# A four-layer graph network on one core: the second layer's parts in one format, its comparisons on another engine, and odd-sized transfers in two

## Chip, cores and metric

The kernel runs on one core of a Trainium2 chip. The metric is device time in microseconds (us) of one execution. The kernel before has a median of 3609.15 us over 3 runs (3607.2 to 3612.18).

The core's engines are named as in the profile: PE (matrix products; PEld is its weight load), DVE (the vector engine), ACT (the scalar engine), POOL (GpSimd) and SP, which here issues transfers. DMA moves data between memory and the on-chip buffers. PSUM is the memory that PE writes its results to.

## What is computed

There are N = 3327 nodes with 512 features, and an adjacency matrix `adj` of N x N. Three attention layers and one aggregation layer follow each other; each reads a normalised, rectified copy of x and is added to x:

```python
h = jnp.maximum(_layernorm(x, axis=-1), 0.0)
x = x + layer(h, adj, ...)
# an attention layer (layers 0 and 2 have 8 heads of 64, layer 1 has 4 heads of 128):
Wh = h @ W                                  # per head
e = leaky_relu(s1[i] + s2[j], 0.2)          # s1, s2: Wh times a vector, per head
attention = softmax(where(adj > 0, e, -inf), over j)
out = elu(attention @ Wh)
# layer 1 alone also sets the diagonal of the mask
# the last layer: mean of the neighbours' features, two dense products, relu
```

## The kernel before

**Tiles.** The nodes make 26 tiles of 128; the last has 127. Targets go in 7 chunks of four tiles (the last chunk has two), sources in five groups `JG` of 6, 6, 6, 4 and 4 tiles.

**Attention without an exponential per edge.** exp(leaky_relu(s1 + s2)) is a product of a factor of the target and a factor of the source, with one pair of factors where s1 + s2 > 0 and another where it is not. So for each head the kernel compares s1 of the chunk's targets with -s2 of every source tile (128 x 512 at a time), which gives a matrix of ones (written as 2.0 in fp8). With the mask it is split into two matrices of edges, and each is multiplied on PE with the source features scaled by the fitting factor (called a = 0 and a = 1). The two sums are scaled per target by `L.c`, added and divided by the last column.

**Where the comparisons run.** In L650 to L657 ACT does them with a huge slope and a Relu (L656), except for the tiles listed in `GP_ON_DVE` (L46), which DVE does (L653): 3 tiles of 26 in the first layer, 8 in the second, 5 in the third. DVE then makes the first matrix by a bitwise "and" with the mask (L662) and the second by an exclusive "or" (L666, in the second layer L722, in place, once the first one has been used).

**Parts.** PE's inputs are split so that the sum keeps float32 accuracy. In layers 0 and 2 the features are three bf16 parts side by side (195 columns, L694 and L697). In the second layer (l = 1) `KIND = "bssvv"` says how each source group goes: group 0 with three bf16 parts (387 columns, L690) and the fp8 matrix as it is; groups 1 to 4 with two float32r parts (258 columns, L687), for which the fp8 matrix is first copied to float32r by `real` (L585): by ACT into buffers "ts" (three of them) for the groups marked s, by DVE into "tv" (two of them) for those marked v. The parts are made by `pieces` or `parts` while the layer before runs, stored to memory and loaded for each head ("ab").

**Order of the second layer.** For each chunk and head: load the scores and parts, make the matrices, then for a = 0 and 1 two passes. A pass takes two target tiles through all 26 source tiles into two of the four accumulators. After a pass DVE reduces the three parts of each accumulator into R (L708; the third is zero where only two were made), and `hooks.run` (L718) lets a step of the next layer's node work in: load x, statistics, normalise, transpose, project, scale, split, store. After the last pass R is multiplied by `L.c` (L730), summed (L732), and divided (L734 to L737).

**Start.** Before the first attention product all 26 tiles are normalised, projected and split (`node_stages` with first=True). x is loaded by SP six tiles ahead (L833), the first layer's weights by SP too (L290), and 20 mask tiles are transposed on PE (L221), written to memory and loaded back (`load_mask`, `mask_tiles`). Then the first head's matrices are made.

**End.** The last layer multiplies the mask with float32r features (L921), adds and stores one tile of `out` at a time (L932).

An order is kept by hand in places: `after(inst, name)` tells the scheduling layer that one instruction is to be placed behind another. All engines take their own instructions in order.

Of the kernel before, what the change touches and what calls it, by code (L numbers as in the profile page):

```python
# [29 lines left out]
FP8 = mybir.dt.float8e4  # L30
F32R = mybir.dt.float32r
# [6 lines left out]
P = 128  # L38
EPS = 1e-5
SLOPE = 0.2  # L40
S_MIN = 1e-35
BIG = 2.0 ** 30
# [3 lines left out]
GP_ON_DVE = [(5, 12, 19), tuple(range(18, 26)), (4, 9, 14, 19, 24)]  # L46


KIND = "bssvv"
# [3 lines left out]
def tile_gnn(ctx: ExitStack, tc: tile.TileContext, x, adj, W0, a01, W1, al, ar, W2, a2,  # L53
# [48 lines left out]
    s1d = [dram.tile([NT, H, P], F32, name=f"s1_{l}") for l, H in enumerate(heads)]  # L102
# [10 lines left out]
    for l in range(3):  # L113
        H, DA, AO, HW = dims(l)
        if l == 1:
            abd.append([dram.tile([H, 2, P, nj, AO], BF16, name=f"ab{l}_{g}") if KIND[g] == "b" else
                        dram.tile([H, 2, P, nj, 2 * DA], F32, name=f"ab{l}_{g}") for g, (_, nj) in enumerate(JG)])
        else:
            abd.append([dram.tile([H, P, nj, HW], BF16, name=f"ab{l}_{g}") for g, (_, nj) in enumerate(JG)])
# [28 lines left out]

    stored = {}
    gone = []  # L150
# [52 lines left out]
    def load_mask(pool, t, g):  # L203


        hooks.done += 1
        n = pn(t)
        c, k = where[t]
        j0, nj = JG[g]
        w = min(nj * P, N - j0 * P)  # L210
        at = pool.tile([P, JM * P], BF16, name="at", bufs=3)
        if n < P:
            nc.vector.memset(at, 0.0)
        elif w < nj * P:
            nc.vector.memset(at[:, w:nj * P], 0.0)
        ld = nc.gpsimd.dma_start(at[:n, :w], adj[t * P:t * P + n, j0 * P:j0 * P + w])
        if gone:
            after(ld, gone[-2] if len(gone) > 1 else stored[NT - 1])
        tp = ps.tile([P, 8, P], BF16, name="tp", bufs=2)
        for j in range(nj):  # L220
            tr = nc.tensor.transpose(tp[:, j, :], at[:, j * P:(j + 1) * P], identb)  # L221
            if j == 0 and gone:
                after(tr, gone[-1])
        st = pool.tile([P, JM, P], FP8, name="st", bufs=3)
        nc.vector.tensor_scalar(st[:, :nj], tp[:, :nj], 0.0, 2.0, op0=ALU.is_gt, op1=ALU.mult, saturate=False)
        if j0 <= t < j0 + nj:
            d = pool.tile([P, P], BF16, name="d", bufs=1)
            nc.vector.tensor_tensor(d, tp[:, t - j0, :], negI, ALU.is_gt)
            nc.vector.tensor_scalar(dg1[:, t, :], d, 2.0, None, op0=ALU.mult, saturate=False)
        nc.sync.dma_start(maskd[c][g][:, k], st[:, :nj])  # L230

    def mask_tiles(c, self_loops=False, early=False):
        t0, nt = chunks[c]
        tiles, loops = [], []
        for g, (j0, nj) in enumerate(JG):
            m = mk.tile([P, PER * JM * P], FP8, name="m")
            v = m[:, :nt * nj * P].rearrange("p (k j i) -> p k j i", k=nt, j=nj)
            ld = nc.sync.dma_start(v, maskd[c][g])
            if early and c == 0:
                after(ld, stored[21])  # L240
            if self_loops:
                for k in range(nt):
                    if j0 <= t0 + k < j0 + nj:
                        loops.append((v[:, k, t0 + k - j0, :].bitcast(U32), dg1[:, t0 + k, :].bitcast(U32)))
            tiles.append(v)
# [17 lines left out]
    def open_layer(l):  # L263
# [17 lines left out]
        for i in range(2):  # L281
            av.append(pre.tile([P, 2, H2, DK], F32, name="h"))
            ld = nc.sync.dma_start(av[i].rearrange("p f h d -> p (f h) d"), a_srcs[l][i].partition_broadcast(P))
            if l:
                after(ld, stored["gate"])
        for k in range(KC):
            for f in range(2):
                dst = L.w[:, k, f, :D // 2]
                if l == 0:
                    nc.sync.dma_start(dst.rearrange("p (g o) -> p g o", g=H2),  # L290
# [6 lines left out]
        def fold(i, k):  # L297
# [3 lines left out]
            if gone:  # L301
                after(m, gone[-1])
            nc.vector.tensor_reduce(L.w[:, k, :, D // 2 + i * H2:D // 2 + (i + 1) * H2], pr, AX.X, ALU.add)
        folds = [lambda i=i, k=k: fold(i, k) for i in range(2) for k in range(KC)]
        if l:
            hooks.small = folds
        else:
            for f in folds:
                f()
# [18 lines left out]
    def normed(xt, mv, pool, behind=None):  # L328
        h = pool.tile([P, D], F32, name="h", bufs=2)
        act = nc.scalar.activation(h, xt, AF.Relu, bias=mv[:, 3:4], scale=mv[:, 2:3])  # L330
        if behind:
            after(act, behind)
        return h
# [7 lines left out]
    def pieces(L, t, AB, pool, first, behind=None):  # L341
# [6 lines left out]
        if o == 0:  # L348
            L.pt = pool.tile([P, H, 2, two, AO] if l == 1 else [P, H, two, HW], BF16, name="pt", bufs=3 if first else 2)
        pt = L.pt  # L350
        nc.gpsimd.memset(pt[:, :, :, o, 3 * DA:AO] if l == 1 else
                         pt[:, :, o].rearrange("p h (a w) -> p h a w", a=2)[..., 3 * DA:AO], 1.0)

        def dst(s, a):
            if l == 1:
                return pt[:, :, a, o, s * DA:(s + 1) * DA]
# [14 lines left out]
        if o == two - 1 and l == 1:  # L371
            for a in range(2):
                L.to_store.append((abd[l][g][:, a, :, js, :].rearrange("h p j w -> p h j w"), pt[:, :, a]))
        elif first and o == two - 1:
# [4 lines left out]
    def projected(L, t, hT, first):  # L379
# [4 lines left out]
        pws = []  # L384
        for f in range(2):
            pw = (accs if first else ps).tile([P, D // 2 + H], F32, name="acc" if first else "mm")
            for k in range(KC):
                L.mm = nc.tensor.matmul(pw, hT[:, k, :], L.w[:, k, f, :], start=(k == 0), stop=(k == KC - 1)).ins.name  # L388
# [3 lines left out]
            pws.append(pw)  # L392
# [19 lines left out]
    def parts(L, t, AB, pool, first, behind=None):  # L412
# [5 lines left out]
        if l == 1 and KIND[g] != "b":  # L418
# [17 lines left out]
    def project_last(L, t, hT, i, behind=None):  # L436
# [10 lines left out]
        if i == 0:  # L447
            def add():
# [4 lines left out]
                nc.sync.dma_start(y1d[c][kk * P:kk * P + n, :], y[:n])  # L453
# [10 lines left out]
    def send_s1(L, t, pool, first):  # L464
# [10 lines left out]
        (nc.sync if first else nc.gpsimd).dma_start(s1d[L.l][t0:t0 + nt].rearrange("t h p -> (t h) p"), s1t[:nt * H])  # L475

    def node_stages(L, t, get_x, pool, first=False):
# [7 lines left out]
        def statistics():  # L485
            q["mv"] = norm(q["x"], pool, behind())
# [21 lines left out]
        if first:  # L508
            return [lambda: (q.update(x=get_x()), statistics(), relu()), turn,
                    lambda: parts(L, t, scaled(L, t, projected(L, t, q["hT"], first), pool, first), pool, first), send]  # L510
# [82 lines left out]
    ahead = {}  # L593

    def load_pieces(L, pool, g, h):
# [4 lines left out]
        v = tl[:, :nj * HW].rearrange("p (j w) -> p j w", j=nj)  # L600
        return v, nc.sync.dma_start(v, abd[L.l][g][h])

    def attention(L, hooks, open_next, close):
# [4 lines left out]
        masks = mask_tiles(0, l == 1, l == 0)  # L608
        for c, (t0, nt) in enumerate(chunks):
            W = nt * P  # L610
# [3 lines left out]
            for h in range(H):  # L614
# [8 lines left out]
                s1b = rp.tile([P, WMAX], F32, name="s1b", bufs=2)  # L623
                nc.sync.dma_start(s1b[:, :W].rearrange("p (k i) -> p k i", k=nt), s1d[l][t0:t0 + nt, h, :].partition_broadcast(P))
                ab = []
                for a in range(2 if l == 1 else 1):
                    row = []
                    for g, (_, nj) in enumerate(JG):
                        if l == 1:
                            tl = mp.tile([P, JM * 2 * DA], F32R, name="ab", bufs=7)  # L630
                            two = KIND[g] != "b"
                            w = 2 * DA if two else AO
                            v = (tl if two else tl.bitcast(BF16))[:, :nj * w].rearrange("p (j w) -> p j w", j=nj)
                            ld = nc.sync.dma_start(v.bitcast(F32) if two else v, abd[l][g][h, a])
                        else:
                            v, ld = ahead.pop(g) if g in ahead else load_pieces(L, mp if l else bp, g, h)
                        row.append(v)
                    ab.append(row)
                if c == 0 and h == 1:
                    stored["gate"] = ld.ins.name  # L640
                    N_ = open_next()
                s1v = s1b[:, :W].rearrange("p (k i) -> p k i", k=nt)
                th, flip = [[], []], []
                for g, (j0, nj) in enumerate(JG):
# [740 lines left out]
```

## Time and profile before

| | us |
|---|---|
| median of 3 runs | 3609.15 |
| the profiled execution | 3609.94 |
| its span, first to last instruction | 3608.10 |
| PE busy | 3470.2 (96%) |
| DVE busy | 2648.6 (73%) |
| ACT busy | 2511.8 (70%) |
| POOL busy | 603.0 (17%) |
| first attention product, layer 0 | at 185.07 |
| first product of the second layer | at 1278.0 |
| last product of the second layer | at 2119.4 |
| last matrix product of all | at 3591.7 |

All numbers of the profile come from one execution, and times in it count from the start of its span. A line of the timeline gives start, length, engine, source line, operation, what is written and read, the size and the number of instructions merged in it; in brackets stands how long the engine was idle before it and what ended that. Lengths of instructions that follow each other overlap by some hundredths of a microsecond, so a rate is read from start to start. A table by stage gives the busy time of each engine in that stretch.

### The profile page before, as it was taken

Reading aid. Unit: us, or ns where it says so; the run is one execution under the profiler, and the core shown is the slowest. Engines: PE = TensorE matmul, PEld = TensorE weight load, DVE = VectorE, ACT = ScalarE, POOL = GpSimd, SP = SyncE. Lnnn points to the kernel's source line nnn. Section 1 sums busy time; section 2 is a strip of 40 time slices with the busy share of each in tenths; the row PEclk is TensorE's granted clock in tenths of the full one; section 3 lists DMA queues with packets and bytes.
Section 4 is the critical chain, followed back from the end, with each engine's and each line's share of the span. In section 5 each row is a group of like instructions: output and inputs, shape, how many; then the busy total and the mean of one; then the engine's idle time right before and its main releaser. Section 6 shows DMA issues by size and latency. Waiting matters only on the chain. (4 is left out here: it accounts for less than half of the span.)

```text
span 3608.1 us, 78551 instructions
## 1 busy us (share of the span) xinstructions
PE 3470.2 (96%) x31291; PEld 3131.4 (87%) x31291; DVE 2648.6 (73%) x5227; ACT 2511.8 (70%) x4113; POOL 603.0 (17%) x855
## 2 busy tenths in 40 slices
PE   6799999999999999999999989999999999999998
PEld 5589999999999878888888869989898989876886
DVE  7688888888887779888888868867676768672211
ACT  5587787777787788888788767767676767572111
POOL 6511221111110111233222230001010101010000
PEclk9899999999999999999999999999999999999999
DMA  7687777878866877877777876655555555576331
GB/s 213 213 239 219 212 217 215 229 207 234 237 194 206 297 264 272 286 254 277 278 257 271 311 265 205 194 176 181 175 191 182 169 176 189 169 270 253 101 104 52
DMA packets 369431, 780.69 MB, mean 216 GB/s; under 512 B 35906, under 2 KB 207333, under 8 KB 368416
## 3 DMA queue, kind: packets, MB, share of 16 engines
q1 hardware_dynamic: 341024, 713.17, 59.4%
q0 software_dynamic: 28032, 62.41, 7.3%
q8 instruction: 249, 4.08, 0.4%
q14 instruction: 126, 1.03, 0.1%
HBM read 667.96 MB, written 129.64 MB: 221 GB/s over the span
## 5 line engine op out<-in xcount | busy, mean ns | idle before, releaser
L694 PE MATMUL acc<-ab,tht 128*128 128x195 bf16 (+1 forms) x10816 | 1840.4, 248 | 15.6 <-DVE tht L662 14.3
L697 PE MATMUL acc<-ab,gt 128*128 128x195 bf16 (+1 forms) x10816 | 1839.4, 248 | 6.6 <-DVE rc L734 4.3
L656 ACT ACTIVATE gt<-s1b,ks 128x512 fp8e4<-128x512 f32 (+1 forms) x2464 | 1457.4, 677 | 316.5 <-issue 158.6
L694 PEld LDWEIGHTS <-tht 128*128 128x128 fp8e4 x10816 | 1059.1, 98 | 28.9 <-DVE tht L662 15.9
L697 PEld LDWEIGHTS <-gt 128*128 128x128 fp8e4 x10816 | 1058.9, 98 | 26.5 <-issue 20.2
L662 DVE TENSOR_TENSOR tht<-gt,m 128x768 uint32<-128x768 uint32 (+3 forms) x560 | 447.4, 799 | 141.4 <-ACT gt L656 139.5
L666 DVE TENSOR_TENSOR gt<-tht,m 128x768 uint32<-128x768 uint32 (+3 forms) x560 | 448.9, 802 | 8.7
L590 ACT CAST ts<-tht 128x1536 fp32r<-128x1536 fp8e4 x208 | 300.3, 1471 | 55.9 <-PE acc L687 51.7
L687 PE MATMUL acc<-ab,ts 128*128 128x258 f32 x2496 | 334.2, 290 | 4.4 <-ACT ts L590 2.3
L653 DVE TENSOR_SCALAR gt<-s1b,ns 128x512 fp8e4<-128x512 f32 (+1 forms) x448 | 222.2, 501 | 149.6 <-PE acc L697 147.9
L687 PEld LDWEIGHTS acc<-ab,ts 128*128 128x128 f32 x2496 | 314.1, 191 | 13.4 <-ACT ts L590 3.0
L921 PE MATMUL acc<-y,mf 128*128 128x512 f32 x1352 | 309.8, 391 | 1.6 <-DVE mf L916 1.6
L656 ACT ACTIVATE tht<-s1b,ks 128x512 fp8e4<-128x512 f32 (+1 forms) x504 | 308.5, 681 | 2.8 <-DMA s1b<-s 2.3
L921 PEld LDWEIGHTS acc<-y,mf 128*128 128x128 f32 x1352 | 253.5, 188 | 57.8 <-DVE mf L916 2.0
L712 DVE TENSOR_REDUCE R<-acc 128x130 f32<-128x390 f32 x416 | 214.5, 555 | 91.6 <-PE acc L697 91.0
L797 POOL TENSOR_TENSOR xt<-xt,e 128x512 f32<-128x512 f32 x72 | 122.2, 1697 | 888.8 <-DVE e L796 567.5
L690 PE MATMUL acc<-ab,tht 128*128 128x387 bf16 x1248 | 226.1, 329 | 6.0 <-DVE tht L662 3.2
L918 ACT CAST mf<-m 128x768 fp32r<-128x768 fp8e4 (+1 forms) x78 | 59.1, 762 | 245.1 <-PE acc L921 233.3
L687 PE MATMUL acc<-ab,tv 128*128 128x258 f32 x1664 | 220.0, 283 | 3.3 <-DMA ab<-ab 2.2
L687 PEld LDWEIGHTS acc<-ab,tv 128*128 128x128 f32 x1664 | 207.5, 189 | 6.2 <-issue 2.1
L388 PE MATMUL mm<-w,hT 128*128 128x260 f32 (+1 forms) x832 | 198.4, 393 | 9.3 <-ACT hT L141 5.6
L690 PEld LDWEIGHTS <-tht 128*128 128x128 fp8e4 x1248 | 117.3, 98 | 83.3 <-DVE tht L662 3.6
(141 smaller groups left out, 3421.4 us busy)
## 6 DMA issues: line engine op xcount, KB each, us to landing
ab<-ab SPq DMA_DIRECT2D x336, 600.0 KB, 5.6
ab<-ab SPq DMA_DIRECT2D x224, 400.0 KB, 4.1
ab<-ab SPq DMA_DIRECT2D x112, 774.0 KB, 6.3
ab<-ab SPq DMA_DIRECT2D x112, 516.0 KB, 5.5
ab<-ab SPq DMA_DIRECT2D x56, 582.0 KB, 6.6
s1b<-s SPq DMA_DIRECT2D x120, 256.0 KB, 6.2
m<-mask SPq DMA_DIRECT2D x72, 384.0 KB, 4.2
ab<-pt SPq DMA_DIRECT2D x13, 1600.0 KB, 7.6
```

The costliest lines, as they stand in the source:

```text
L388: L.mm = nc.tensor.matmul(pw, hT[:, k, :], L.w[:, k, f, :], start=(k == 0), stop=(k == KC - 1)).ins.name
L590: (nc.scalar.copy if KIND[g] == "s" else nc.vector.tensor_copy)(t[:, :k1 - k0, :nj], th[a][g][:, k0:k1])
L653: nc.vector.tensor_scalar(gv[:, :, jj, :], s1v, L.ns2[:, j, h:h + 1], 2.0, op0=ALU.is_gt, op1=ALU.mult, saturate=False)
L656: nc.scalar.activation(gv[:, :, jj, :], s1v, AF.Relu, bias=L.ks2[:, j, h:h + 1], scale=BIG, saturate=False)
L662: nc.vector.tensor_tensor(pu, gu, mu, ALU.bitwise_and)
L666: nc.vector.tensor_tensor(gu, pu, mu, ALU.bitwise_xor)
L687: mm = nc.tensor.matmul(acc[k][:, :2 * DA], thr[g][:, k - ks[0], jj, :], ab[a][g][:, jj, :], start=(j == 0), stop=(j == NT - 1), skip_grou ...
L690: mm = nc.tensor.matmul(acc[k][:, :3 * DA], th[a][g][:, k, jj, :], ab[a][g][:, jj, :3 * DA], start=(j == 0), stop=(j == NT - 1), skip_grou ...
L694: nc.tensor.matmul(acc[k][:, :3 * DA + o], th[0][g][:, k, jj, :], ab[0][g][:, jj, :3 * DA + o], start=(j == 0), stop=False, skip_group_che ...
L697: mm = nc.tensor.matmul(acc[k][:, AO:AO + 3 * DA + o], th[1][g][:, k, jj, :], ab[0][g][:, jj, AO:AO + 3 * DA + o], start=False, stop=(j == ...
L712: nc.vector.tensor_reduce(R[:, k], v.rearrange("p a (s d) -> p a d s", s=3), AX.X, ALU.add)
L921: nc.tensor.matmul(acc[k], mf[:, jj, :], y2[g][:, jj, s, :], start=(j0 + jj == 0 and s == 0), stop=(j0 + jj == NT - 1 and s == 1))
```

## The change

1. **One format in the second layer.** `KIND` becomes "vssvv": group 0 has two float32r parts like the others. `real` makes its float32r matrix on DVE in a "tv" buffer; these stay two and grow from 4 to 6 source tiles each. The "tht" buffers of that layer go from 10 to 9. `parts`, the stores and the loads follow.
2. **Sums scaled out of PSUM.** In the second layer the reduce, the product with `L.c` and the sum are replaced by two operations for each accumulator, which scale each part by the target's factor and add it to R. `close_terms`, which makes the factors, comes before the first of them.
3. **Comparisons.** In the second layer the eight source tiles that DVE compared become tiles 1, 4, 7, 10, 13, 16, 19, 23, and POOL compares them. It writes the byte 64, which read as fp8 is 2.0.
4. **Transfers of 127 rows.** `move` issues a transfer of a row count that 16 does not divide as two: 112 and 15 rows here. It is used for loads of x, for y1, for the last layer's rows and for the store of `out`.
5. **Start.** The first chunk's masks are written straight into the buffers that attention reads, group by group; a mask tile's load is issued one step before its transposes. x is loaded by ACT's queue from the third tile on, half of the first weights too, and the statistics of the first two tiles come before the products with the attention vectors. Tiles 0 and 1 are projected first without their score columns. The first head's parts are copied on the chip into the buffers that attention reads. The first head's scores are loaded and the matrices of groups 0 to 2 made during the projections (`early`).
6. **Next layer's weights** are opened at the fourth head of the first chunk instead of the second, in layers 0 and 2.

The core of the diff:

```diff
-GP_ON_DVE = [(5, 12, 19), tuple(range(18, 26)), (4, 9, 14, 19, 24)]
-KIND = "bssvv"
+ELSEWHERE = [(5, 12, 19), (1, 4, 7, 10, 13, 16, 19, 23), (4, 9, 14, 19, 24)]
+KIND = "vssvv"
...
+    def move(eng, to, src, n):
+        m = n - n % 16
+        ld = eng.dma_start(to[:m], src[:m])
+        return [ld] if m == n else [ld, eng.dma_start(to[m:n], src[m:n])]
...
+            if j in ELSEWHERE[l] and l == 1:
+                nc.gpsimd.tensor_scalar(gv[:, :, jj, :].bitcast(U8), s1v, L.ns2[:, j, h:h + 1], TWO,
+                                        op0=ALU.is_gt, op1=ALU.mult, saturate=False)
+            elif j in ELSEWHERE[l]:
+                nc.vector.tensor_scalar(gv[:, :, jj, :], s1v, L.ns2[:, j, h:h + 1], 2.0,
+                                        op0=ALU.is_gt, op1=ALU.mult, saturate=False)
...
                             if l == 1:
-                                nc.vector.tensor_reduce(R[:, k, a, :], acc[k][:, :3 * DA].rearrange("p (s d) -> p d s", s=3),
-                                                        AX.X, ALU.add)
+                                cf = L.c[:, t0 + k, a, h:h + 1]
+                                for s in range(2):
+                                    v = acc[k][:, s * DA:(s + 1) * DA]
+                                    if a == s == 0:
+                                        nc.vector.tensor_scalar(R[:, k, 0, :], v, cf, None, op0=ALU.mult)
+                                    else:
+                                        nc.vector.scalar_tensor_tensor(R[:, k, 0, :], v, cf, R[:, k, 0, :],
+                                                                       op0=ALU.mult, op1=ALU.add)
...
-                Rv = R[:, :nt]
-                nc.vector.tensor_mul(Rv, Rv, L.c[:, t0:t0 + nt, :, h:h + 1].to_broadcast([P, nt, 2, DA]))
-                nc.vector.tensor_add(num[:, :nt], Rv[:, :, 0, :], Rv[:, :, 1, :])
+                if l != 1:
...
-            [A[1], ("ab", JM * 258, F32R, 7), R, ("ts", 2 * JM * P, F32R, 3), ("tv", 2 * 4 * P, F32R, 2), tht[:3] + (10,)],
+            [A[1], ("ab", JM * 258, F32R, 7), R, ("ts", 2 * JM * P, F32R, 3), ("tv", 2 * JM * P, F32R, 2), tht[:3] + (9,)],
...
-                nc.sync.dma_start(xt[:pn(u)], x_rows(0, u))
+                for ld in move(nc.scalar if u > 1 else nc.sync, xt, x_rows(0, u), pn(u)):
+                    if relus:
+                        after(ld, relus[-1])
...
+            for g in range(3):
+                if n == (8, 15, 21)[g]:
...
+                    pv, gv, _, steps = matrices(L, PER, 0, g, early["s1"], masks0[g], b[:, :s], b[:, s:2 * s])
+                    hooks.small += steps
+                    early[g] = pv, gv
...
-                    nc.sync.dma_start(out[t * P:t * P + n, :], o[:n])
+                    move(nc.sync, out[t * P:t * P + n, :], o, n)
```

## The prediction, made before the changed kernel was run

> **What bounds the kernel now.** I read the page's table of 40 slices first, then busy time by stage, then PE's timeline inside the second layer, then what waits at the two ends of the run. By stage (start to first attention product, layer one, layer two, layer three, aggregation, tail):
>
> ```profile
> 0.00:185.00 185.00, 128.97 (x631) 104.48 (x631) 121.51 (x253) 105.52 (x223) 110.94 (x193) 0.92 0.71 211
> 185.00:1278.00 1093.00, 1065.51 (x11933) 1037.34 (x11933) 904.18 (x1844) 858.50 (x1514) 174.56 (x273) 0.99 0.77 225
> 1278.00:2120.00 842.00, 826.36 (x5943) 719.78 (x5944) 729.63 (x1373) 705.91 (x964) 206.61 (x230) 0.99 0.79 279
> ...
> 3592.00:3608.00 16.00, 0.00 (x0) 0.00 (x0) 1.19 (x2) 0.00 (x0) 0.00 (x0) 0.62 0.06 19
> ```
>
> The columns are the stretch, then busy us of PE, weight loads, DVE, ACT and POOL, then granted clock, DMA share, GB/s. PE is busy 98% of layer two (826 of 842 us) and DVE 87%: PE is the bound, DVE is close behind. The first 185 us and the last 16 us are not PE-bound. One pass (two target tiles, 26 source tiles) of layer two:
>
> ```profile
> 1613.84 2.14 PE L690 MATMUL acc<-ab,tht 128*128 128x387 bf16 x12
> 1615.68 3.19 PE L687 MATMUL acc<-ab,ts 128*128 128x258 f32 x24
> 1618.71 2.08 PE L687 MATMUL acc<-ab,tv 128*128 128x258 f32 x16
> 1620.63 2.15 PE L690 MATMUL acc<-ab,tht 128*128 128x387 bf16 x12
> ```
>
> From start to next start a pass is 6.79 us. The 16 "tv" products start 0.120 apart (1.92/16). At 0.120 for all 40 float32r products, the 12 bf16 ones take 6.79 - 4.80 = 1.99, or 0.166 each.
>
> **Layer two on PE.** The 1248 bf16 products of 387 columns become float32r ones of 258. At 0.120 a pass is 52 x 0.120 = 6.24: 0.55 less. Read the other way, by the "ts" spacing (3.03/24 = 0.126), the 12 take 1.51 instead of 1.84: 0.33 less. There are 26 tiles / 2 x 4 heads x 2 parts = 104 passes, so 34 to 57 us; single starts in the middle of each run are 0.164 and 0.120 apart, which gives 0.52 a pass. I take **-54 us** of PE time.
>
> **Layer two on DVE, per head of four tiles.** The window 1400 to 2000 holds 19 heads (152 "tv" copies, 8 a head) of 31.6 us; DVE is busy 525.7 us in it, 27.7 a head. Durations below are start to start, so about 0.08 less than a row's. Removed: 8 reduces of R (row 0.55) 3.8; 8 comparisons at L653 (0.48) 3.3; the product with cpm (1.22) 1.1; the sum of R (0.68) 0.6: 8.8. Added: 4 copies of 1536 elements, each 0.60 of a 1024 copy plus 512 more at that copy's rate, 0.88: 3.5; 16 scalings of 129 columns from PSUM, of which no row exists: between the 8-column PSUM operation (0.16) and a third of the reduce's stream plus its start (0.29), near the latter, 0.21 each: 3.4. DVE comes to 27.7 - 8.8 + 6.9 = 25.8.
>
> **Layer two on POOL.** Eight comparisons a head, 128x512 with one tensor input, 8-bit out. No row shows that: bounds are the one-column TENSOR_SCALAR (0.23 shortest) and the two-input 512-column add (1.26 shortest); I take 0.9, nearer the row of the same width, 7.2 us a head. POOL is busy 8 us a head now, so it fits; and tht buffers let it run most of a head ahead, four of five groups at least. What it does to DVE is in the trace:
>
> ```profile
> 1606.27 2.63 POOL L367 TENSOR_TENSOR pt<-r 128x520 bf16<-128x520 f32 x2 [14.17 <-DVE r L359]
> ```
> ```profile
> 1606.10 0.68 DVE L590 CAST tv<-tht 128x1024 fp32r<-128x1024 fp8e4 x1
> 1606.70 2.87 DVE L653 TENSOR_SCALAR tht<-s1b,ns 128x512 fp8e4<-128x512 f32 x3
> ```
>
> Three comparisons that take 1.3 us elsewhere take 2.87 while POOL runs; at 1663.89 POOL's add takes 4.59 behind DVE's words. They take turns. In the window POOL's work, at its unhindered durations, is 100 us, and DVE's operations exceed their usual durations by 32 us: 0.32 lost per us of POOL. By that, 7.2 us cost DVE 2.3 a head (28.1 in all); at twice that rate, 4.6 (30.4). PE's head becomes 31.6 - 2.1 = 29.5, so DVE is 95 to 103% loaded.
>
> The Trainium skill ("SBUF — State Buffer", section Who interferes with whom) speaks against the change: GpSimd and a VectorE operation that reads through both ports, or has two SBUF inputs, exclude each other for the whole instruction. The trace agrees (comparisons 1.27 to 1.51 instead of 0.48). The skill's "GPSIMD Engine Reference", section 3.1, gives 769 ns for a tight one-input loop over 512 elements; if all of that blocked, layer two would lose 8 x 0.77 x 28, about 170 us of DVE time (an estimate from that page), and with the measured share 55. Nothing else here uses these figures.
>
> **A new wait.** "tv" keeps two buffers but serves three groups a pass now (0, 3, 4). So the copy of group 0 for the next pass waits until PE has used up group 3, and PE has only group 4's 8 products, 0.96 us, before it needs that copy. The copy itself is 0.96, the handovers about 0.2 and 0.1 (a tv copy at 1619.87 starts 0.2 after group 3's last product): 0.3 us of stall at best. Behind that waiting copy on DVE stand the scalings, which free the accumulators, and the copies of groups 3 and 4. Of 104 gaps, 26 hold a projection (3.55 us) and hide it, 26 four transposes (0.44), 52 nothing: 52 x 0.3 = 16 us. In the built order DVE's work between two such copies is 4 to 9 us around a mean of 6.1, and DVE can't work ahead past the wait; with the losses above I add 0.4 for each of the 78 poorly covered passes, 31 us (0 to 75). Layer two: -54 + 16 + 31 = **-7 us**, bounds -41 (57 saved) and +37 (75 added).
>
> **The start.**
>
> ```profile
> 117.76 0.30 SPq L833 DMA_DIRECT2D xt<-in_x_dram  x1
> ...
> 131.81 0.69 DVE L318 BATCH_NORM_STATS2 st<-xt 128x6 f32<-128x512 f32 x1 [10.70 <-DMA xt<-in_x_dram]
> ```
> ```profile
> PE acc L694 <- DVE tht L662: 8.6, 1, 8.6
> ```
>
> The 127-row load of x takes 14 us, where 128 rows land in 4.7 (median). It stops DVE for 10.7 us, and PE for 11.4. In two parts it arrives in time: -10. PE then waits 8.6 us at 176.5 for the first head's matrices; groups 0 to 2 are now made during the projections (18 comparisons, 15 of them on ACT at 0.7), and group 3 is still to come: -6. The first product starts at 18.05 since POOL's scale factors stand behind its weight products (first at 10.67); the built order has them in front, and the weight loads, 6.5 us of issue on one queue, go by two: -5 (0 to -8). Against that, 15 comparisons and the x loads' issues now share ACT with the hT copies that PE waits for in its 4.94 us loop: +3 (0 to 8). The local copy of the pieces replaces four loads of about the same size. Together **-18 us**, bounds -10 and -26.
>
> **The tail.**
>
> ```profile
> 3592.53 0.69 DVE L931 SCALAR_TENSOR_TENSOR o<-o,xo 127x512 f32<-127x512 f32 x1
> 3593.25 0.25 SPq L932 DMA_DIRECT2D out_dram<-o  x1
> ```
> ```profile
> out_dram<-o SPq DMA_DIRECT2D x25, 256.0 KB, 2.7
> ```
>
> The last store, 127 rows, moves one 2 KB packet every 0.08 us at 26 GB/s until 3605.6, 12 us after its issue; the 25 stores of 128 rows land in 2.7. As 112 and 15 rows it needs that and one more issue: **-9 us** (-8 to -10). The other 127-row moves (y1, xo, x between layers) lie beside PE work; their stall at layer ends is within 2 us.
>
> **Beside other work, taken as nothing.** Group 0's parts grow from 582 to 774 KB a load, 11 MB more in 842 us (1.5% at a DMA share of 0.79); PE waits 4.3 us on such loads now, so 0 to +10. Weights opened at the fourth head, mask loads one step earlier, 9 instead of 10 tht buffers: hidden by PE work, -5 to +8. Layers one and three are otherwise unchanged.
>
> **Sum.** 3609.94 (this execution; span 3608.10 and 1.84 around it) - 18 - 9 - 7 = **3576**. The execution is 0.8 above the median of 3609.15, so against the median it is 33 less.
>
> **Rivals.**
> - DVE keeps up and PE sets the pace: the comparisons run in gaps and only the handover stays, -54 + 16 = -38: 3609.94 - 18 - 9 - 38 = **3545**. For: POOL's adds wait while DVE is dense, and PSUM scalings leave the pair free. Against: DVE's 95%. 27%.
> - DVE becomes layer two's bound through POOL's turns: slower. With 1.0 us lost for each comparison DVE needs 25.8 + 8.0 = 33.8 a head, 2.2 over today's 31.6; 26 heads' worth of tiles give +57: 3609.94 - 27 + 57 = **3640**. It decides from 32.6 a head (31.6 + 27/26), or 0.85 us lost per comparison. At the upper bound, 1.26 all lost, 25.8 + 10.1 gives 3694. For: L737 rows of 1.1 us instead of 0.28 next to POOL. 20%.
> - The start does not shorten (the work put into it delays hT as much as the load did) and layer two comes out even or a little over: 3609.94 - 9 + 5 = **3606**, no change. 8%.
>
> The forecast has the remaining 45%. Faster by over 0.2% (7.2 us, about what a measurement of this kernel tells from no change): 45 + 27 = 72%; within it 8%; slower 20%. The range goes from 7 below the fast rival (its start at the -25 end) to just below the slower rival's 3640, so that about half of that rival (10%) and the low end of the fast one (10%) stay outside: 3538 to 3636.
>
> **What would show it.** Right: bn statistics of the last tile without a 10 us wait, first attention product near 167, last packet within 4 us of its issue, layer-two passes of 6.2 to 7.0 us, POOL comparisons of 0.8 to 1.0. Wrong: tv copies that often wait on POOL, gaps over 1 us in front of group 0's products (slower rival), or passes of 6.3 us throughout (fast rival).

## The result and the profile after

The changed kernel takes 3698.09 us (median of 4 runs, 3696.43 to 3712.39), the kernel before 3610.66 us beside it: ratio 1.0256, 95% interval 1.0243 to 1.0269. The forecast was 3576, faster; the time lies above its range. The profiled execution took 3696.43 us, its span 3694.6.

The view by stage of the changed kernel (start to first attention product, layer one, layer two, layer three, aggregation, tail; columns as before: stretch, busy us of PE, weight loads, DVE, ACT and POOL, granted clock, DMA share, GB/s):

```profile
0.00:161.20 161.20, 129.41 (x662) 108.27 (x663) 126.39 (x246) 105.40 (x224) 111.86 (x183) 0.95 0.76 218
161.20:1289.70 1128.50, 1076.79 (x11935) 1047.07 (x11933) 906.24 (x1856) 852.34 (x1502) 177.50 (x269) 0.98 0.75 222
1289.70:2210.20 920.50, 814.77 (x5937) 778.24 (x5938) 751.67 (x1403) 708.12 (x963) 715.92 (x452) 0.95 0.74 265
...
3686.10:3694.60 8.50, 0.35 (x2) 0.00 (x0) 1.44 (x2) 0.00 (x0) 0.00 (x0) 0.64 0.13 36
```

Beside the spans of before, with the same marks:

| stage | before | after | difference | forecast |
|---|---|---|---|---|
| start | 185.1 | 161.2 | -23.9 | -18 |
| layer one | 1093.0 | 1128.5 | +35.5 | 0 |
| layer two | 841.4 | 920.5 | +79.1 | -7 |
| layer three, aggregation | 1471.9 | 1475.9 | +4.0 | 0 |
| tail, from the start of the last product to the end | 16.8 | 8.5 | -8.3 | -9 |

The differences add up to 86.4; the spans differ by 86.5. In layer two PE is busy 89% now instead of 98%, while POOL went from 207 to 716 us. No engine is full: DVE is at 82%, ACT at 77%, POOL at 78%. The reason for POOL's figure stands in its costliest group:

```profile
L644 POOL TENSOR_SCALAR tht<-s1b,ns 128x512 uint8<-128x512 f32 (+1 forms) x224 | 512.0, 2296 | 110.9 <-ACT ts L619 80.6 <-issue 17.9 <-DMA s1b<-s 6.6
```

A comparison takes 2.30 us in the mean over both widths (512 columns, and 256 in the last chunk), 2.44 at full width alone; the shortest of full width took 1.98. The forecast took 0.9, between 0.23 and 1.26.

Who waits in layer two (us in total, times, longest):

```profile
PEld acc L737 <- DVE tv L619: 84.7, 62, 6.6
POOL tht L644 <- ACT ts L619: 80.6, 25, 6.3
...
PE acc L737 <- DVE tv L619: 63.4, 39, 6.3
...
DVE tht L654 <- POOL tht L644: 30.3, 22, 2.5
```

PE waits for DVE's copies of matrices, DVE for POOL's comparisons, and POOL for buffers that are free once ACT has copied them: the wait goes round. (PEld and PE tell of the same gaps.) The timeline shows such a gap:

```profile
1428.10 11.48 POOL L644 TENSOR_SCALAR tht<-s1b,ns 128x512 uint8<-128x512 f32 x5
...
1432.90 0.96 DVE L654 TENSOR_TENSOR tht<-tht,m 128x768 uint32<-128x768 uint32 x1 [2.50 <-POOL tht L644]
...
1433.78 1.37 DVE L619 CAST tv<-tht 128x1536 fp32r<-128x1536 fp8e4 x1
...
1435.20 2.95 PE L737 MATMUL acc<-ab,tv 128*128 128x258 f32 x12 [4.85 <-DVE tv L619]
```

POOL compares from 1428.10 on, DVE stands 2.50 us until a comparison is there, applies the mask and only then makes group 0's float32r copy, which stands behind it, and PE stands still for 4.85 us in front of group 0's products, the sign that the forecast named for its slower rival. Not every gap is of this kind:

```profile
1582.74 4.97 DVE L778 TENSOR_TENSOR tht<-tht,m 128x768 uint32<-128x768 uint32 x4
...
1583.70 2.00 POOL L854 TENSOR_TENSOR xt<-xt,e 128x512 f32<-128x512 f32 x1
...
1588.64 2.44 PE L737 MATMUL acc<-ab,tv 128*128 128x258 f32 x12 [3.06 <-DVE tv L619]
```

Here no comparison runs. Group 0's copy stands on DVE behind four exclusive-ors, which take 4.97 us while POOL does additions that it did before the change too. Five gaps of this kind (at 1454, 1589, 1726, 1863 and 1998) make 16 of the 106 us that PE is idle in the layer.

The two ends went about as forecast. The last store of the changed kernel, behind the last sum:

```profile
3687.27 0.69 DVE L1015 SCALAR_TENSOR_TENSOR o<-o,xo 127x512 f32<-127x512 f32 x1
3687.99 0.33 SPq L154 DMA_DIRECT2D out_dram<-o  x1
3688.38 0.86 SPq L155 DMA_DIRECT2D out_dram<-o  x1
```

The span ends at 3694.6, 6.6 us after the first issue; before, it ended 14.9 us after the issue of the 127-row store (3608.1 - 3593.25). In the start no statistics wait 10 us for x any more (3.0 us for x in all).

### The profile page after: what moved, and what is told of

It reads as the page before. It is cut to its first block, busy times and chain, and to the rows that moved or that the text cites. A ratio compares the mean times of both kernels' runs of the same rounds, so it can differ in the third digit from the quotient of the medians.

```text
span 3694.6 us, 79030 instructions
## 1 busy us (share of the span) xinstructions
PE 3472.7 (94%) x31323; PEld 3205.6 (87%) x31323; DVE 2677.5 (72%) x5265; ACT 2507.7 (68%) x4101; POOL 1124.5 (30%) x1064
## 5 line engine op out<-in xcount | busy, mean ns | idle before, releaser
L744 PEld LDWEIGHTS <-gt 128*128 128x128 fp8e4 x10744 | 1055.5, 98 | 27.0 <-issue 19.7
L741 PEld LDWEIGHTS <-tht 128*128 128x128 fp8e4 x10744 | 1055.7, 98 | 20.1 <-DVE tht L654 7.3
L644 POOL TENSOR_SCALAR tht<-s1b,ns 128x512 uint8<-128x512 f32 (+1 forms) x224 | 512.0, 2296 | 110.9 <-ACT ts L619 80.6
L737 PE MATMUL acc<-ab,tv 128*128 128x258 f32 x2912 | 419.9, 298 | 94.9 <-DVE tv L619 63.4
L737 PEld LDWEIGHTS acc<-ab,tv 128*128 128x128 f32 x2912 | 385.7, 200 | 111.5 <-DVE tv L619 84.7
L854 POOL TENSOR_TENSOR xt<-xt,e 128x512 f32<-128x512 f32 x72 | 107.9, 1499 | 824.6 <-DVE e L853 591.2
L647 DVE TENSOR_SCALAR gt<-s1b,ns 128x512 fp8e4<-128x512 f32 (+1 forms) x446 | 221.2, 500 | 164.6 <-PE acc L744 161.2
L619 DVE CAST tv<-tht 128x1024 fp32r<-128x1024 fp8e4 (+1 forms) x312 | 274.5, 889 | 88.9 <-PE acc L737 88.0
L737 PE MATMUL acc<-ab,ts 128*128 128x258 f32 x2496 | 326.0, 288 | 1.8 <-ACT ts L619 1.4
L336 POOL TENSOR_SCALAR mv<-mv 128x1 f32<-128x1 f32 x104 | 51.2, 492 | 639.9 <-DVE mv L335 533.1
```

The source lines that it names most:

```text
L619: (nc.scalar.copy if KIND[g] == "s" else nc.vector.tensor_copy)(t[:, :k1 - k0, :nj], th[a][g][:, k0:k1])
L644: nc.gpsimd.tensor_scalar(gv[:, :, jj, :].bitcast(U8), s1v, L.ns2[:, j, h:h + 1], TWO, op0=ALU.is_gt, op1=ALU.mult, saturate=False)
L647: nc.vector.tensor_scalar(gv[:, :, jj, :], s1v, L.ns2[:, j, h:h + 1], 2.0, op0=ALU.is_gt, op1=ALU.mult, saturate=False)
L737: mm = nc.tensor.matmul(acc[k][:, :2 * DA], thr[g][:, k - ks[0], jj, :], ab[a][g][:, jj, :], start=(j == 0), stop=(j == NT - 1), skip_grou ...
L741: nc.tensor.matmul(acc[k][:, :3 * DA + o], th[0][g][:, k, jj, :], ab[0][g][:, jj, :3 * DA + o], start=(j == 0), stop=False, skip_group_che ...
L744: mm = nc.tensor.matmul(acc[k][:, AO:AO + 3 * DA + o], th[1][g][:, k, jj, :], ab[0][g][:, jj, AO:AO + 3 * DA + o], start=False, stop=(j == ...
```

## The experiments

A first theory, A: the comparisons on POOL cost most of layer two's 79 us. The rival, B: the two "tv" buffers that now serve three groups do. C: layer one's loss comes from the mask loads, which wait for the pass just before and not for the one before that. "Before" of the same chip was 3608.6 to 3613.9 in the three batches.

**Comparisons back on DVE.**

```diff
-            if j in ELSEWHERE[l] and l == 1:
+            if False:
```

> The changed kernel (3696.4 us in its profiled execution, layer two 920 us) with the second layer's eight comparisons a head back on DVE; all else as changed. Theory A (the comparisons on POOL, 2.0 us each unhindered, hold DVE up, and DVE is then late with group 0's copy): layer two falls to 800 to 840 us, the whole to about 3580 to 3616. Theory B (two tv buffers for three groups a pass are the cause, whoever compares): layer two stays above 890, the whole above 3665.

Measured: 3645.15 us, ratio 1.0087 (1.0064 to 1.011); layer two 869.0. The comparisons on POOL cost 52 us of the 79, and another 28 has another cause. The measured values lie between the spans of the two theories: A's cause is the larger one, but not the only one.

**Five buffers instead of 3 + 2.**

```diff
-        t = mp.tile([P, 2, nj, P], F32R, name="ts" if KIND[g] == "s" else "tv", bufs=3 if KIND[g] == "s" else 2)
+        t = mp.tile([P, 2, nj, P], F32R, name="tt", bufs=5)
```

> The changed kernel with its three ts and two tv buffers made one set of five (the same memory), so that each group's float32r copy waits only for the same group one pass earlier; POOL still compares. Theory B: the waits in front of group 0's products go, layer two about 800 us, the whole about 3580. Theory A: DVE is still slowed by POOL but may now run ahead, so only part comes back: layer two 850 to 890, the whole 3625 to 3665.

Measured: 3671.17 us, 1.0155 (1.0125 to 1.0184); layer two 897.2. The handover is worth 23 us. B falls as the main cause; what is left is more than A's span allowed for, too.

**The kernel before, with its layer-two comparisons from DVE on POOL.**

```diff
-                        if j in GP_ON_DVE[l]:
+                        if j in GP_ON_DVE[l] and l == 1:
+                            nc.gpsimd.tensor_scalar(gv[:, :, jj, :].bitcast(U8), s1v, L.ns2[:, j, h:h + 1], 64.0,
+                                                    op0=ALU.is_gt, op1=ALU.mult, saturate=False)
+                        elif j in GP_ON_DVE[l]:
```

> The kernel before (3609.9 us) with only the comparisons of the second layer moved to POOL (the same tiles 18 to 25, byte 64 as fp8), its bf16 group 0, two tv buffers for two groups and the old sums kept. Theory A: POOL's turns cost DVE, which has no more than 12% to spare there: slower by 20 to 60 us. Theory B: POOL's comparisons alone cost nothing, within 7 us of before.

Measured: 3787.42 us, 1.0476 (1.0446 to 1.0507). That is 174 us more than the kernel before beside it, where 20 to 60 were expected: this one edit alone costs more than the whole change. (It puts all comparisons of the last two source groups on POOL, tiles 18 to 25; the change spreads its eight over all groups. So the two costs are not to be subtracted from each other.) Its layer two:

```profile
1279.40:2297.60 1018.20, 877.18 (x5937) 748.70 (x5938) 679.46 (x1148) 708.97 (x964) 659.40 (x453) 0.93 0.64 231
```

It is 1018 us long where the kernel before needs 841, and no engine but PE with its weight loads is over 70% busy. A second thing is to be seen: PE does exactly the products of before, but is busy 877 us with them and not 826. The mean granted clock is 0.93 here and 0.99 there. In the records of both runs the clock is either full or half, and half in stretches of 3.4 us or a multiple of it: 146 us of this layer, 14 us before. Half of PE's busy time in those stretches is 50 us here and 6 before, which is 44 of the 51 us. So gaps on PE (141 us here) are paid again through the clock of the products behind them. The changed kernel shows it at the second gap above:

```profile
1585.90:1589.30 3.40, 0.66 (x5) 0.66 (x6) 3.40 (x8) 3.40 (x5) 0.82 (x2) 1.00 0.99 294
1589.30:1592.70 3.40, 3.40 (x18) 3.40 (x17) 3.19 (x8) 3.37 (x5) 1.76 (x1) 0.50 1.01 407
1592.70:1600.00 7.30, 6.78 (x56) 6.58 (x56) 6.25 (x12) 5.28 (x7) 6.69 (x8) 1.00 0.90 366
```

After 3.4 us in which PE was busy for 0.66, the clock is 0.50 for 3.4 us and 18 products take all of them (0.19 each); then it is full and a product takes 0.12. The Trainium skill ("TensorE: Matmul & The Clock Gate", Part 1: The HAM clock gate) says that the array's clock is gated down to half after an idle window of about 3.4 us and released by activity. The trace agrees on the half and on the 3.4 us, but the stretch ahead need not be idle throughout: each of the 20 half-clock stretches of the changed kernel's second layer began after 3.4 us with 1.8 us or more of idle time on PE, while other gaps, the longest of 2.3 us, had none behind them. The forecast had no term for it.

**Mask loads one pass earlier, as before the change.**

```diff
-            after(ld, gone[-1] if gone else stored[NT - 1] if c else relus[-3])
+            after(ld, (gone[-2] if len(gone) > 1 else gone[-1]) if gone else stored[NT - 1] if c else relus[-3])
```

> The changed kernel, but a mask tile's load in the first layer is ordered behind the last but one pass, as before, not behind the last. Theory C (the 23 us that layer one lost are PE waiting for mask loads issued in the same pass as their transposes): PE's waits at the mask transposes, 8 of 4 to 5.6 us, go, the whole falls by 20 to 30 us to about 3670. Rival D (layer one lost them at its start, where the first head now has less work ahead): no change within 7 us.

Measured: 3669.43 us, 1.015 (1.0121 to 1.018); layer one 1097.1 instead of 1128.5. C holds: 28.7 us in all. Layer one's waits of the changed kernel name the line:

```profile
PE tp L235 <- DMA at<-in_adj_dram: 31.6, 8, 5.4
```

In the kernel before the same wait is this, and with the loads moved back none is left:

```profile
PE tp L221 <- DMA at<-in_adj_dram: 4.6, 2, 4.2
```

**Both suspects of layer two taken away together** (the first two edits).

> The changed kernel with both suspects of layer two taken away together: VectorE compares all tiles there, and the shares of the five groups stand in five buffers, so that group 0's copy waits for its own group of the pass before only. With VectorE's comparisons alone layer two took 869 us (28 over before's 841), with five buffers alone 897. Theory H (what is left after the comparisons is the handover of the two tv buffers): layer two 800 to 825 us, time 3575 to 3602. Theory V (what is left is VectorE's own work: four copies of 1536 and sixteen scalings a head that take 0.30 each start to start instead of 0.21): layer two 850 to 869, time 3626 to 3645, and PE's gaps stand behind VectorE's copies and scalings.

Measured: 3623.36 us, 1.0032 (1.0018 to 1.0045); layer two 854.2. Layer two is in theory V's span, not in H's, and the time 3 us below V's. V's sign is met in part only: PE's waits name copies by DVE (14.3 us) and by ACT (12.2), loads of parts (10.6) and no releaser that the profile shows (14.4). Most of the 79 us is gone, yet layer two is still no shorter than before the change.

**The same with the mask loads back.**

> The kernel of the run above (VectorE compares, five buffers) with layer one's mask loads behind the pass before the last, as before the change. That alone saved 28 us of the changed kernel, in layer one. Theory C, the mask loads' cost adds to the others: 24 to 30 us less than the run above. If the stages share the loss (a layer one that ends sooner meets a stall later), less than 15.

Measured: 3593.69 us, 0.9944 (0.9927 to 0.9961): 29.7 less, so this cost adds to the others.

**The changed start, tail and transfers around the old layer two.** KIND back to "bssvv", the reduces and the product with `L.c` back, comparisons on DVE, mask loads as before.

> The changed kernel's start, tail and two-part transfers, with before's whole second layer (bf16 parts for group 0, sums by one product and one reduce, VectorE compares) and the mask loads one pass earlier. If the start's 24 us and the tail's 8 are the change's only gains and reach the end unshortened: 3611 - 24 - 8 = 3579; where layer one takes back 11 us as in the run with the mask loads moved (1097 instead of 1093, and a layer two that began only 13 us sooner): 3586 to 3594. Rival: layer two, beginning elsewhere in its load pattern, gives it back: 3605 or more.

Measured: 3577.9 us, 0.9901 (0.9884 to 0.9918), the fastest of all versions that leave nothing out, and as expected in the first of the three cases. In its profile the start is 19.8 us shorter and the tail 8.4, layer one 2.6 shorter and layer two 1.9 longer: the gains of the two ends reach the end unshortened.

**What makes a comparison take 2 us.** Seven forms on scratch memory in the last stage, one line of this kind each:

```diff
+            nc.gpsimd.tensor_scalar(out_at(0, 1).bitcast(U8), gs, gq, 64.0, op0=ALU.is_gt, op1=ALU.mult, saturate=False)
+            nc.gpsimd.tensor_scalar(out_at(3, 4).bitcast(F32), gs, gq, 2.0, op0=ALU.mult, op1=ALU.mult)
```

> The kernel before, with 42 extra GpSimd operations on scratch memory in the last stage (seven forms, each 128x512, one SBUF tensor in, each on a line of its own): greater-than against a column and times a constant to 8-bit; the same to float32; greater-than alone to float32; product with a column and a constant to float32; product with one constant to float32; greater-than and times a constant to bf16; plain copy to float32. Theory O (the 8-bit output makes the 2.0 us): 2.0 for the first alone, 0.5 to 1.0 for the others. Theory S (the second operation of the chain does): 2.0 for all with two operations, 1.0 to 1.3 for those with one. Theory P (the operand that is a column per partition does): only the product with one constant and the plain copy are near 1. The time of the kernel itself rises by no more than 90 us.

Measured (3611.25 us in its one run, beside 3610.41 of the kernel before; group rows: busy us, mean ns; L915, L916 and L920 compare and multiply, L917 only compares, L918 is the product with a column and a constant, L919 the product with one constant):

```profile
L920 POOL TENSOR_SCALAR gap<-gap 128x512 bf16<-128x512 f32 x6 | 12.4, 2073 | 0.0
L916 POOL TENSOR_SCALAR gap<-gap 128x512 f32<-128x512 f32 x6 | 12.2, 2037 | 0.0
L915 POOL TENSOR_SCALAR gap<-gap 128x512 uint8<-128x512 f32 x6 | 12.2, 2034 | 0.1
L917 POOL TENSOR_SCALAR gap<-gap 128x512 f32<-128x512 f32 x6 | 10.1, 1683 | 0.0
L919 POOL TENSOR_SCALAR gap<-gap 128x512 f32<-128x512 f32 x6 | 9.6, 1599 | 0.0
L918 POOL TENSOR_SCALAR gap<-gap 128x512 f32<-128x512 f32 x6 | 4.6, 763 | 0.0
```

None of the three theories: neither the output's type (O) nor the second operation (S) nor the column (P). L918 has two operations and a column and is the fast one (median 0.69; one of the six was slow and lifts the mean); the plain copy took 0.61.

**Only the two-part load of x and store of the output, on the kernel before; and more forms.**

```diff
-                nc.sync.dma_start(xt[:pn(u)], x_rows(0, u))
+                move(nc.sync, xt, x_rows(0, u), pn(u))
...
-                    nc.sync.dma_start(out[t * P:t * P + n, :], o[:n])
+                    move(nc.sync, out[t * P:t * P + n, :], o, n)
```

> The kernel before with only two of the change's edits: the 127-row load of x and the 127-row store of the output go in two parts. Besides, seven more GpSimd forms on scratch memory in the last stage (the first seven cost that stage nothing). By the forecast's terms the load is worth 10 at the start and the store 9 at the end (8.2 measured): 3610 - 18 = 3592. If the start's other edits are needed for the load's gain to reach the end: 3602. Forms: the first seven gave 2.0 us for greater-than and times a constant whatever the output, 1.6 for greater-than alone, 1.5 for the product with one constant, but 0.69 for the product with a column and a constant. If the product is what makes a form fast, product with column and constant to 8-bit stays below 0.9 and sum with column above 1.4; if a column as operand does, sum, difference and product with a column are all below 1 and only comparisons are slow.

Measured: 3591.81 us, 0.9954 (0.994 to 0.9968). First attention product at 174.0 (11.1 sooner), from the start of the last product to the end 8.3. Three of the forms (L924: difference, then maximum; L920: product of column and constant to 8-bit; L923: sum with the column, then product):

```profile
L924 POOL TENSOR_SCALAR gap<-gap 128x512 f32<-128x512 f32 x6 | 12.2, 2029 | 0.0
...
L920 POOL TENSOR_SCALAR gap<-gap 128x512 uint8<-128x512 f32 x6 | 4.2, 693 | 0.1
L923 POOL TENSOR_SCALAR gap<-gap 128x512 f32<-128x512 f32 x6 | 4.1, 688 | 0.0
```

Sum or product alone with the column took 1.6, greater-than against a constant and then product 1.9, the difference as an operation on two tensors 1.0. So it is neither the product nor the column that makes a form fast. Of the one-tensor forms tried only the plain copy and two chained sums or products are short, at 0.61 and 0.69; with a comparison or a maximum in a chain of two it is 1.9 to 2.0 in the median, whatever the output.

**VectorE's load: the first of four scalings on ACT**, on the version with DVE's comparisons, five buffers and early mask loads.

```diff
-                                        nc.vector.tensor_scalar(R[:, k, 0, :], v, cf, None, op0=ALU.mult)
+                                        nc.scalar.activation(R[:, k, 0, :], v, AF.Copy, scale=cf)
```

> The kernel with VectorE's comparisons, five buffers and early mask loads (3593.7 us, layer two 852, VectorE busy 790 of it and ScalarE 703), and the first of each tile's four scalings out of PSUM done by ScalarE: four a head, 104 in all, 0.30 us less each on VectorE (31 us). Theory V (VectorE's load is what keeps PE waiting there): layer two 825 to 845, time 3567 to 3586. Rival, the gaps come from the order of the engines' work and not from VectorE's sum, or ScalarE's copies now come late: layer two 850 or more.

Measured: 3584.47 us, 0.9935 (0.9919 to 0.9952), but layer two is 851.1 long (852.3 without the edit): DVE fell from 790 to 764 us (0.25 a scaling, not 0.30) and nothing came of it there: that is the rival's size. DVE now waits 12.1 us for ACT's scalings (L764 on L762). The time is in theory V's span, but by the ratios (0.9935 here, 0.9944 without the edit) the two kernels don't differ beyond their intervals; the profiled execution, 3590.35, was the slowest of four.

**Half the scalings left out.**

```diff
-                                for s in range(2):
+                                for s in range(1):
```

> The same kernel (VectorE compares, five buffers, early mask loads) without the scalings of each product's second 129 columns, so that the low parts of the result are left out: eight operations a head fewer on VectorE, 208 x 0.30 = 62 us. Theory V: PE's idle time in layer two falls from 63 us to 30 or less, layer two 805 to 825, time 3547 to 3566. Rival, order and not load: idle time stays above 50 and layer two above 840.

Measured: 3560.11 us, 0.9869 (0.9849 to 0.9889); layer two 827.8, PE idle 46.7. DVE fell by 47 us, layer two by 25, PE's idle time by only 16. The time is in theory V's span, layer two 3 us above it, and the idle time is between the two theories: DVE's load counts, at about half its value, and about three quarters of the idle time (46.7 of 62.6) stay without it.

**The changed kernel with a short form in place of POOL's comparison.**

```diff
-                                        op0=ALU.is_gt, op1=ALU.mult, saturate=False)
+                                        op0=ALU.mult, op1=ALU.mult, saturate=False)
```

> The changed kernel with the comparison's greater-than on GpSimd replaced by a product (column and constant, 8-bit out), a form that took 0.69 us with float32 out: the attention's entries of those tiles are no comparisons any more, so the result is another one, and only the time is of use. Theory A, the comparison's price was the mis-sized term: with 0.7 to 0.9 us (the forecast's 0.9) GpSimd's work in layer two falls from 716 to about 420, layer two to 850 to 875 and the time to 3630 to 3655, near the kernel whose comparisons are on VectorE (3645). Rival P, it is the shared access of the two engines and not the length: layer two stays above 900. Were the 8-bit output slow for products, GpSimd's operation stays at 2 us and the run tells nothing more than the changed kernel did.

Measured: 3649.78 us, 1.0116 (1.0099 to 1.0133). The row and layer two:

```profile
L644 POOL TENSOR_SCALAR tht<-s1b,ns 128x512 uint8<-128x512 f32 (+1 forms) x224 | 210.3, 949 | 184.4 <-ACT ts L619 157.3 <-DVE tv L619 12.8 <-DMA s1b<-s 8.2
```

```profile
1293.90:2171.60 877.70, 802.00 (x5937) 763.63 (x5938) 740.21 (x1403) 708.53 (x963) 449.68 (x451) 0.97 0.79 279
```

The mean is 0.95, nearly the forecast's 0.9, and everything else is the change's. The time is in theory A's span, layer two 3 us above it, and POOL is busy 450 us, not 420. Layer two falls by 43 us to 878: that much hung on the length of the operation. Rival P (shared access, whatever the length) falls. But 878 is not the forecast's 834 either, and it is longer than with the comparisons on DVE (869).

## Why the prediction was wrong

Layer two by version. The last column is PE's busy time less half of that part of it in which the clock was at half, so the products' length at full clock; before and "before, comparisons on POOL" have the same products and differ by 7 us, which is how far it can be trusted:

| version | layer two | PE busy | PE idle | clock | at full clock |
|---|---|---|---|---|---|
| before | 841.4 | 825.8 | 15.6 | 0.99 | 820 |
| before's layer two, new ends | 843.3 | 823.6 | 19.7 | 1.00 | 820 |
| before, comparisons on POOL | 1018.2 | 877.2 | 141.0 | 0.93 | 827 |
| after | 920.5 | 814.8 | 105.7 | 0.95 | 775 |
| after, five buffers | 897.2 | 798.9 | 98.3 | 0.95 | 771 |
| after, short form on POOL | 877.7 | 802.0 | 75.7 | 0.97 | 778 |
| after, DVE compares | 868.9 | 797.2 | 71.7 | 0.97 | 774 |
| ... and five buffers, mask loads | 852.3 | 789.7 | 62.6 | 0.97 | 766 |
| ... and first scaling on ACT | 851.1 | 793.0 | 58.1 | 0.96 | 767 |
| ... or half the scalings out | 827.8 | 781.1 | 46.7 | 0.98 | 763 |

- **The PE term, -54: right within its bounds of 34 and 57.** At full clock the products became 45 us shorter in the changed kernel and 42 to 57 in the others.
- **The failed step: "Layer two on POOL", "I take 0.9, nearer the row of the same width", in bounds of 0.23 and 1.26.** The comparison takes 2.0 us undisturbed and 2.4 in layer two, beyond the upper bound. The bounds were rows of other operations; the width did not decide, the kind of operation did. With a form of 0.95 in its place the layer is 43 us shorter. The Trainium skill gives 769 ns for a tight one-input loop over 512 elements ("GPSIMD Engine Reference", section 3.1). That is near the forms with two chained sums or products (0.69) and far from those with one such operation (1.5 to 1.6) or with a comparison and a product (2.0): here the measurement decides.
- **The loss on DVE through POOL's turns, +2.3 a head: right in sum, by luck.** Between 1400 and 2000 DVE's operations exceed their usual durations (the shortest fifth of each kind) by 71 us in the changed kernel (212 "tv" copies, 12 a head, are 17.7 heads) and by 32 before (19 heads): 4.0 a head instead of 1.7, 2.3 more. But the eight comparisons are 16 us of POOL at their undisturbed length and not 7.2, so the loss is 0.14 per us of POOL and not 0.32: two misses that cancel. The slower rival had the right sign and sign-posts, but not the mechanism: DVE did not become full (752 of 920 us). That its upper figure, 3694, is next to the measured 3696 is luck too; it rests on a full DVE and has nothing for layer one's 35.5 us. What grew was the round of waits: POOL's comparison late, then DVE's mask product and copy, then PE, and only then POOL's next buffer. That the round is what stretches is read from the waits; the runs show its price, not each of its links.
- **The handover of two "tv" buffers, +16, and the uneven passes, +31.** Five buffers bring 23 us with POOL comparing, 15 with DVE. In the run with the short form PE's idle time is 75.7; the forecast's 15.6 + 16 + 31 is 63. So the two terms together were 13 us short for the price that they were made with; no run tells the second one apart.
- **A term that was missing: the clock.** In the run with the short form layer two is 43 us longer than forecast: idle time 13, the products 12 (42 us saved, not 54), and the clock 18 (half of PE's busy time at half clock is 24 us there, 6 before). In the changed kernel: idle time +90, clock +34, products -45 give the +79.
- **The scalings, "0.21 each": 0.26 start to start** (the row says 342 ns). The bound taken for the upper end, 0.29, was nearer. Sixteen a head make +0.8 us of DVE; by the run with half of them left out such time counts by about half. The expectations of three runs above say 0.30, which is too long.
- **"Mask loads one step earlier ... hidden by PE work, -5 to +8": wrong, +29.** A load was ordered behind the pass just ended, and where two mask steps follow one pass, its transposes came behind the same pass, so that PE waited for it; before the change the load stood one pass ahead. The forecast read the step's move in the order and missed that its release had come nearer to its use.
- **Group 0's larger loads, 0 to +10.** Their 11 MB are not 1.5% but 4.7% of what layer two moves (279 GB/s for 841 us). PE waits 23.6 us for loads of parts in the changed kernel, 7.1 before. With the short form it is 4.5 and with DVE comparing 2.3, so the size of the loads is not the reason; how the late comparisons lead to it is not shown.
- **The start, -18: right, -23.9 in the changed kernel.** The x load alone brings 11.1 (10 forecast). The bounds given, -10 and -26, don't follow from the terms, which give -8 to -24; nothing hangs on that. In the other versions with the changed start the first attention product comes at 161.4 to 168.2, so 17 to 24 us sooner, also where nothing was edited but the second layer; the cause of that spread is not shown. **The tail, -9: right, -8.3.**

The sum of the misses on the profiled execution: start -6, layer one +35.5, layer two +86, later stages +4, tail +1 make 120, which is 3696 - 3576. The comparison's price accounts for 43 of it, the order of the mask loads for 29.

The old layer two with the new ends gives 3577.9; the new layer two, with DVE comparing, five buffers and early mask loads, gives 3593.7. So the new layer two did not pay even without its two large faults: 54 us saved on PE's products at full clock went into 47 us of idle time and 17 of the lower clock. Whether that is the float32r parts or the sums scaled out of PSUM is not told apart: no run has the new parts with the old sums, and with half the scalings left out the layer is 14 us shorter than before. Why PE still waits 47 us there stays open. The waits name ACT's copies (18.7 us) ahead of DVE's (7.1); with all scalings it was 11.2 and 17.3, and moving work from DVE to ACT turned it to 18.7 and 13.0 without a gain.

## What to carry to other kernels

An operation that no row of the profile shows is not bounded by rows of other operations of the same width: time the exact form by itself on scratch memory in an idle stage, which cost nothing here (3611.25 against 3610.41), before it is put on a path. Where PE is 98% busy and its helpers are at 84 to 87%, work saved on PE is only worth something if every helper's hand-over comes sooner too, and gaps are paid a second time through the clock. When a load is re-ordered, count the time from its new release to its use, not its place in the list.

## What the runs showed of the hardware

- POOL's one-input TENSOR_SCALAR of 128x512: 0.69 us with two chained sums or products, 1.5 to 1.6 with only one such operation, 1.6 for a comparison alone, 1.9 to 2.0 for a comparison and a product or a difference and a maximum (medians of six each). A second operation can make it faster than one alone.
- The granted clock followed PE's gaps in the second layer: 0.99 to 1.00 with 16 to 20 us of idle time, 0.96 to 0.98 with 47 to 76, 0.95 with 98 to 106, 0.93 with 141, whichever format the products had. It was full or half; in the changed kernel each of 20 half-clock stretches of 3.4 us (or a multiple) began after 3.4 us with at least 1.8 us of idle time.
- A 127-row store as 112 and 15 rows ended 8.3 us after the start of the last product instead of 16.8, in the kernel before with only its 127-row load of x and this store in two parts.
